# A graph convolution on one core: two chunks fetch their rows before the branch

## The chip, the cores and the metric

The kernel runs on one core of a Trainium2 chip. The metric is the device time in microseconds (us) from the kernel's start to its end on that core. The engines are called PE (TensorE, matmuls), DVE (VectorE), ACT (ScalarE), POOL (GpSimd) and SP (SyncE). Each has its own queue of instructions and works through it in order; they wait for each other by semaphores. SP, ACT and POOL also issue DMA transfers.

## The reference

Two graph convolutions with attention over 6250 nodes of 128 features and 106250 edges sorted by destination, a batch normalisation with ReLU between them, and a layer norm of the sum with x at the end. Each edge has 64 attributes, a weight that serves as a time, and a source whose node has a time of its own:

```python
def _transformer_conv(h, edge_attr, src, dst, ...):
    q, k, v = (h @ Wq + bq), (h @ Wk + bk), (h @ Wv + bv)      # each (n, H=2, C=64)
    e = (edge_attr @ We).reshape(-1, H, C)
    kj = k[src] + e
    alpha = einsum('ehc,ehc->eh', q[dst], kj) / sqrt(C)
    ex = exp(alpha - segment_max(alpha, dst)[dst])
    a = ex / segment_sum(ex, dst)[dst]
    out = segment_sum((v[src] + e) * a[:, :, None], dst)
    return out.reshape(n, H * C) + h @ Ws + bs

rel_t = last_update[src] - t                                    # node_vec[src] - edge_weight
edge_attr = concatenate([cos(rel_t[:, None] * time_w + time_b), msg], axis=-1)
h = relu(batch_norm(_transformer_conv(x, edge_attr, ..conv 1..)))
return layernorm(x + _transformer_conv(h, edge_attr, ..conv 2..))
```

## The kernel before, in words

The edges are cut into 104 chunks of 1024 (`NC`, `CE`), each of 8 tiles of 128 edges (`T`). Since the edges are sorted, a chunk's destinations lie in a window of 64 nodes (`NN`), in four groups. A tile `ff` of a chunk holds, for each edge, the source's time (column 0), the source's 128 features, 32 encoded times, 64 attributes and 16 bits that mark the destination.

The program has a plan and a branch. The plan (`tile_gnn_resnorm`, L1355 to L1521) loads source and destination indices as rows, checks that the edges are sorted and narrow enough (the result is `oki`, L1505), loads all features into SBUF (`load_features`), writes them back to DRAM with the node's time in front as `xv_d` (`pass_features`, L530 to L533), turns index rows into columns (`columns`, L1428 to L1434: `srcs`, `dsts`, `ew`), multiplies weights (`matrices`, L583 to L604), and makes the first block of the table of queries and skips (`tables`, L630 to L642, from `x0`). DVE works in this order: source columns, plan check, destination columns, matrices, table, edge weight columns. Then every engine reads `oki` and branches: `ordered` if the plan holds, `general` otherwise, which doesn't run here.

`ordered` first turns all features (`turn_features`, L656 to L662: 13 groups of transposes by PE, evacuated alternately by DVE and ACT), then runs `conv(0)` and `conv(1)`. In `conv` the order of all instructions is written out by hand, round by round; round k works on several chunks at once:

- `fetch` (L777 to L807) issues on SP the loads of a chunk ahead: attributes, tables, skips; DVE writes the bits.
- `gather` (L815) issues on POOL, per tile of the chunk, one indirect DMA of 128 rows: of `xv_d` in the first convolution, of the first one's output in the second. `bring` calls it; from round -1 on most of the eight gathers have `behind`, an extra wait for a step of PE in the same round. In the first convolution chunk k + 4 (`AHEAD`) is fetched and gathered in round k, so rounds -4 to -2 gather chunks 0 to 2 without such a wait.
- `encode` and `sine` (L853 to L867) make the encoded times of chunk k + 2 from column 0 of `ff` and the edge weights.
- `turn_in` (L885 to L897) transposes chunk k + 1; `score` (L916) makes the scores of chunk k; `lowest` (L924) takes their minimum, one instruction a round; `weigh`, `turn_weights`, `gather_sums` (L956) and `divide` to `complete` finish the chunks before.
- `pull(extra, n)` takes n steps of side work from a generator (`rest`): further blocks of the table, the second convolution's matrices, storing of outputs.

The chunk tiles `ff` come from a pool of 7 in the first convolution and of 6 in the second.

Of the kernel before, what the change touches and what calls it, by code (L numbers as in the profile page):

```python
# [15 lines left out]
H = 2  # L16
# [48 lines left out]
SWITCH = NC - 3  # L65
STARTS = (*range(0, NC - 2, LG), NC - 2, NC - 1)
# [3 lines left out]
def general(ctx: ExitStack, tc: tile.TileContext, x, src, dst, edge_attr_64, edge_weight, node_vec,  # L70
# [95 lines left out]
    step = RW * GT * (-(-64 // GT))  # L166
# [147 lines left out]
    def conv(c, kv_d, qt_d, agg_d):  # L314
        we = wt[c][4]
        w = 2 * D + (c == 1)
        with ExitStack() as cs:
            load = cs.enter_context(tc.tile_pool(name=f"load{c}", bufs=3))
# [327 lines left out]
def turn_features(nc, pl, mp, N):  # L646

    xT = pl.xT
    NF = pl.rows.shape[1]
    nc.vector.memset(xT[:, N:], 0.0)  # L650
    lanes = xT[:, :NF * P].rearrange("d (p b) -> d b p", b=NF)
    for b0 in range(0, NF, 4):
        n = min(4, NF - b0)
        px = mp.tile([P, 4, P], F32, name="fpx")
        for i in range(n):
            nc.tensor.transpose(px[:, i], pl.rows[:, b0 + i, 1:], pl.ident)  # L656
        eng = nc.scalar.copy if b0 // 4 % 2 else nc.vector.tensor_copy
        eng(lanes[:, b0:b0 + n], px[:, :n])
    if N > NF * P:
        px = mp.tile([P, 4, P], F32, name="fpx")  # L660
        nc.tensor.transpose(px[:, 0], pl.rest[:, 1:], pl.ident)
        nc.vector.tensor_copy(xT[:, NF * P:N], px[:, 0, :N - NF * P])  # L662
# [3 lines left out]
def ordered(ctx: ExitStack, tc: tile.TileContext, pl, x, dst, edge_attr_64, conv2, bn_g, bn_b, out):  # L666
# [9 lines left out]
    const = ctx.enter_context(tc.tile_pool(name="fconst", bufs=1))  # L676
    dram = ctx.enter_context(tc.tile_pool(name="fdram", bufs=1, space=bass.MemoryType.DRAM))
# [51 lines left out]
    AHEAD = 4  # L729

# [9 lines left out]
    def conv(c, extra, first_blocks=None):  # L740
# [27 lines left out]
        def fetch(k):  # L768
# [9 lines left out]
            s.f = f = load.tile([P, T, FW], F32, name="ff")  # L778
# [31 lines left out]
        def gather(k, rows, behind=None):  # L810
            f = ch[k].f
            for t in rows:
                if k == NC - 1 and t > whole:
                    continue
                row = nc.gpsimd.indirect_dma_start(  # L815
                    out=f[:, t, (1 if c else 0):1 + D], out_offset=None, in_=(h_d[:N, :] if k < RAW else hn_d) if c else pl.xv_d,
                    in_offset=bass.IndirectOffsetOnAxis(ap=pl.srcs[:, t, k:k + 1], axis=0))
# [26 lines left out]
        def encode(k):  # L844
# [8 lines left out]
            nc.vector.tensor_sub(rel, s.f[:, :, 0], pl.ew[:, :, k])  # L853
# [205 lines left out]
        with cs, tc.manual_schedule():  # L1059
            ended = None  # L1060
            for k in range(-lead(-NC), NC - 2 if c else NC + 3):
# [138 lines left out]
    with tc.tile_pool(name="fpw", bufs=2) as pw:  # L1200
        with tc.tile_pool(name="ftp", bufs=3, space=bass.MemoryType.PSUM) as mp, tc.manual_schedule():
            turn_features(nc, pl, mp, N)

# [34 lines left out]
        def rest():  # L1238
# [4 lines left out]
            others = second()  # L1243
            targets()
# [99 lines left out]
def tile_gnn_resnorm(ctx: ExitStack, tc: tile.TileContext, x, src, dst, edge_attr_64, edge_weight, node_vec,  # L1344
# [11 lines left out]
    with tc.tile_pool(name="plan", bufs=1) as pl, tc.tile_pool(name="planw", bufs=2) as mw, \  # L1356
# [4 lines left out]
        nc.gpsimd.memset(got.hT[:, N // P * (1 + D):], 0.0)  # L1361
        got.rest = keep.tile([P, 1 + D], F32, name="fxrest")
# [30 lines left out]
        got.bs1 = load_column(nc.scalar, keep, "fbs1", conv1["bs"])  # L1393
        got.wv = [keep.tile([P, D], F32, name=f"fwv{c}") for c in (0, 1)]
# [30 lines left out]
        def columns(t, to):  # L1425
# [4 lines left out]
            for t0 in range(0, T, 4):  # L1430
# [3 lines left out]
                nc.vector.tensor_copy(to[:, t0:t0 + 4], pt)  # L1434

        columns(srows, srcs)
        passed = pass_features(nc, got, made, N)

# [60 lines left out]
        x0 = pl.tile([P, GE // P, D], F32, name="fx0")  # L1499
        nc.scalar.dma_start(x0, x[:GE, :].rearrange("(b p) d -> p b d", p=P))  # L1500
        rows(nc.scalar, erows, edge_weight, CE)
# [58 lines left out]
```

## Time and profile before

| | us |
|---|---|
| median of 3 runs | 2671.73 (2668.62 to 2673.74) |
| profiled execution | 2670.95 |
| its span, first to last instruction | 2669.1 |
| PE busy | 1851.4 |
| POOL busy | 1588.3 |
| DVE busy | 1148.0 |
| ACT busy | 1082.5 |

A row of the profile's timeline gives start and duration in us from the span's start, the engine (PEld is PE's weight load; SPq and ACTq are DMA issues of these queues), the line, the operation, the tile written and the tiles read, the shape and how often; the brackets hold the idle time of the engine before it and what ended it. "issue" means that the profile shows nothing that it waited for, "remote" a releaser that the profile doesn't know. A group's row gives busy time and the mean in ns of one.

### The profile page before, as it was taken

The numbers are of one execution on the slowest core, as the hardware profiler recorded it, in microseconds if no ns is written. First come the engines' busy times: TensorE is split into PE (matmuls) and PEld (weight loads), VectorE is DVE, ScalarE is ACT, GpSimd is POOL, SyncE is SP. The second block draws the span as 40 slices with busy tenths as digits, with TensorE's granted clock in tenths as the row PEclk, the third lists the DMA queues.
The fourth block names the chain that finished last, engine by engine and source line by source line (L and its number), as shares of the span: only waits on it lengthen the run. The fifth ranks groups of instructions, "written<-read, shape, count | busy, mean of one in ns | idle before, by whom it ended". The sixth has DMA issues, their size and how long they took to land. (4 is left out here: it accounts for less than half of the span.)

```text
span 2669.1 us, 50291 instructions
## 1 busy us (share of the span) xinstructions
PE 1851.4 (69%) x14961; PEld 1107.9 (42%) x14961; DVE 1148.0 (43%) x3998; ACT 1082.5 (41%) x1906; POOL 1588.3 (60%) x1684
## 2 busy tenths in 40 slices
PE   3677767777777677677746667676767767676666
PEld 2444444444444444444424334444444434443443
DVE  3555555555555555565625222333232322232223
ACT  1455545553434444454532333333333333333333
POOL 4466666666666666666345666666666666666662
PEclk8799889988989989889977888888888898888888
DMA  6455555555555555555447555555555555555542
GB/s 177 128 148 146 146 153 145 144 143 151 146 147 138 152 148 145 144 144 138 126 118 194 148 140 148 152 153 147 143 150 148 157 147 142 154 143 140 128 134 52
DMA packets 535244, 383.29 MB, mean 144 GB/s; under 512 B 405638, under 2 KB 479258, under 8 KB 531634
## 3 DMA queue, kind: packets, MB, share of 16 engines
q1 hardware_dynamic: 460998, 231.66, 33.4%
q0 software_dynamic: 53184, 109.45, 17.1%
q10 hardware_dynamic: 20780, 38.87, 3.9%
q8 instruction: 122, 2.00, 0.3%
q14 instruction: 160, 1.31, 0.2%
HBM read 267.85 MB, written 108.49 MB: 141 GB/s over the span
## 5 line engine op out<-in xcount | busy, mean ns | idle before, releaser
L815 POOL DMA_INDIRECT ff<-xv_d,fsrcs x831 | 795.1, 957 | 511.2 <-issue 166.2
L815 POOL DMA_INDIRECT ff<-hn_d,fsrcs x783 | 743.6, 950 | 453.3 <-issue 172.3
L941 ACT COPY fpt<-fppt 128x384 f32<-128x384 f32 x208 | 99.6, 479 | 1261.9 <-PE fpx L885 705.6
L916 PE MATMUL fps<-fft,ftab 128*32 128x384 f32 (+2 forms) x2080 | 406.2, 498 | 146.5 <-issue 64.5
L956 PE MATMUL fpa<-ff,fpt 128*32 128x225 f32 x5008 | 350.6, 419 | 120.0 <-DVE fres L1032 102.2
L924 DVE TENSOR_REDUCE flow<-fps 128x1 f32<-128x384 f32 x208 | 116.1, 558 | 587.6 <-PE fpx L885 352.7
L885 PE MATMUL fpx<-fident,ff 128*128 128x128 f32 x1664 | 276.9, 299 | 38.5 <-issue 25.8
L956 PEld LDWEIGHTS fpa<-ff,fpt 128*32 128x32 f32 x5008 | 167.6, 125 | 321.0 <-issue 233.7
L916 PEld LDWEIGHTS fps<-fft,ftab 128*32 128x32 f32 x2080 | 142.7, 124 | 323.6 <-issue 161.8
L894 PE MATMUL fpe<-fident,ff 128*112 128x128 f32 x832 | 142.4, 295 | 189.0 <-issue 184.3
L889 ACT COPY fft<-fpx 128x512 f32<-128x512 f32 x404 | 232.2, 575 | 45.7 <-remote 20.1
L885 PEld LDWEIGHTS fpx<-fident,ff 128*128 128x128 f32 x1664 | 221.0, 156 | 54.5 <-issue 36.1
L916 PE MATMUL fps<-fxT,ftab 112*32 112x384 f32 (+2 forms) x1040 | 218.4, 509 | 17.2 <-issue 16.8
L963 DVE TENSOR_SCALAR finv<-fpa 128x1 f32<-128x1 f32 x208 | 32.0, 154 | 446.8 <-PE fps L916 237.6
L916 PE MATMUL fps<-fet,ftab 112*32 112x384 f32 (+2 forms) x1040 | 167.4, 448 | 33.0 <-issue 32.7
L894 PEld LDWEIGHTS fpe<-fident,ff 128*112 128x112 f32 x832 | 97.1, 141 | 218.6 <-issue 213.1
L978 PE MATMUL fpa<-fsel,fa 128*128 128x128 f32 x416 | 103.3, 332 | 81.5 <-DVE fsel L968 46.5
L860 DVE SCALAR_TENSOR_TENSOR farg<-fturns,farg 128x256 f32<-128x256 f32 x312 | 132.9, 426 | 10.7
L895 ACT COPY fet<-fpe 112x512 f32<-112x512 f32 x208 | 124.6, 599 | 9.9 <-PE fps L916 2.8
L940 PE MATMUL fppt<-fident,fs 128*128 128x128 f32 x626 | 117.1, 296 | 13.4 <-issue 5.8
L931 ACT ACTIVATE fs<-fps,fm 128x384 f32<-128x384 f32 x208 | 120.5, 579 | 9.7 <-DVE fm L926 6.1
L867 ACT ACT_TABLE_LOAD x82 | 105.2, 1283 | 42.2 <-issue 34.7
(224 smaller groups left out, 2654.4 us busy)
## 6 DMA issues: line engine op xcount, KB each, us to landing
ff<-in_edge_attr SPq DMA_DIRECT2D x206, 256.0 KB
et_d<-fet SPq DMA_DIRECT2D x104, 448.0 KB
fxT<-et_d SPq DMA_DIRECT2D x104, 448.0 KB
tab_d<-fo ACTq DMA_DIRECT2D x26, 1024.0 KB
ftab<-tab_d SPq DMA_DIRECT2D x832, 32.0 KB
enc_d<-fzs SPq DMA_DIRECT2D x104, 128.0 KB
fz<-enc_d SPq DMA_DIRECT2D x104, 128.0 KB
ff<-xv_d,fsrcs POOLq DMA_INDIRECT x831
```

Source lines behind the costliest of these rows:

```text
L815: row = nc.gpsimd.indirect_dma_start(out=f[:, t, (1 if c else 0):1 + D], out_offset=None, in_=(h_d[:N, :] if k < RAW else hn_d) if c else ...
L860: nc.vector.scalar_tensor_tensor(arg, turn, -part, arg, op0=OP.mult, op1=OP.add)
L867: nc.scalar.activation(z[:, :len(of)], arg[:, :len(of)], AF.Sin, bias=qpi)
L885: last = nc.tensor.transpose(px[:, t * P:(t + 1) * P], s.f[:, u * 4 + t, 1:1 + D], ident)
L889: nc.scalar.copy(s.ft[:, u * GE:(u + 1) * GE], px)
L894: last = nc.tensor.transpose(pe[:EC, t * P:(t + 1) * P], s.f[:, u * 4 + t, 1 + D:], ident)
L895: nc.scalar.copy(s.et[:, u * GE:(u + 1) * GE], pe[:EC])
L916: steps.append(nc.tensor.matmul(s.ps[r, to:to + n], s.tab[:kd, r, i], (of.et if i else of.ft)[:kd, at:at + n], start=i == 0, stop=i == 1))
L924: nc.vector.tensor_reduce(low, s.ps, AX.X, OP.min)
L931: nc.scalar.activation(s.s[:, :s.ps.shape[1]], s.ps, AF.Exp, bias=s.bias, scale=-1.0)
L940: last = nc.tensor.transpose(pp[:, t * P:(t + 1) * P], s.s[:, t * P:(t + 1) * P], ident)
L956: steps.append(nc.tensor.matmul(s.pa[r], s.pt[:, t * P + g * GH:t * P + (g + 1) * GH], f[:, i % T, 1:1 + D + EW], start=t == 0, stop=t == ...
```

## The change

Chunks 0 and 1 (`EARLY`) get tiles of their own, allocated for the whole program. As soon as the source columns stand, POOL gathers their 16 tiles of rows from x itself, so without the node's time, ahead of the branch and of `xv_d`. `gather` then leaves these two out.

The times that are missing are picked in the plan by `early_times`. node_vec lies in 98 rows of 64 (`SLOT`). For each of the 2 x 1024 edges PE spreads the source index over 98 lanes, ACT squares its distance from each lane's centre, DVE compares, which gives a one-hot column; PE multiplies it with node_vec's rows, and DVE multiplies with a one-hot of the low six bits and sums. This goes in 4 units (2 chunks x 2 halves of 512 edges), one after each of the first four steps of `tables`. `encode` reads the result for these chunks.

In the plan DVE now does the check, then the matrices, the preparation of the picked times, the code, the table with the units between its steps, the edge weight columns and the destination columns last. The load of `x0` on ACT's queue moves up, ahead of the loads of edge weights.

`turn_features` no longer stands ahead of the first round: it is a generator at the head of the side work, of which 3 steps are taken in rounds -2 and -1 and 7 more in round 0. In the first convolution gathers have no `behind` up to round 2, so chunks 3 to 6 are gathered without PE's pace as well. The other five chunk tiles are allocated once, in two pools (`upper` for chunks 2 and 3, `lower` for 4 to 6), and both convolutions use the ring of 7. Two buffer sizes in `general` shrink.

```diff
+AHEAD = 4
+EARLY = 2
+SLOT = 64
...
+def early_times(nc, pl, keep, plan, mw, rowf, node_vec, wide):
+
+    N = node_vec.shape[0]
+    n = -(-N // SLOT)
+    of = plan.tile([P, SLOT], F32, name="fslots")
+    nc.vector.memset(of[n // 32 * 32:], 0.0)
+    nc.scalar.dma_start(of[:N // SLOT], node_vec[:N // SLOT * SLOT].rearrange("(p b) -> p b", b=SLOT))
+    if N % SLOT:
+        nc.scalar.dma_start(of[n - 1:n, :N % SLOT], node_vec[N // SLOT * SLOT:].rearrange("(a b) -> a b", a=1))
+    centre = plan.tile([P, 2], F32, name="fcentre")
+    nc.vector.tensor_copy(centre[:, 0:1], pl.lanes)
+    nc.vector.tensor_scalar(centre[:, 1:2], centre[:, 0:1], -float(SLOT), 0.5 - SLOT / 2, op0=OP.mult, op1=OP.add)
+    row = plan.tile([EARLY, P], F32, name="frow")
+    nc.vector.tensor_copy(row, pl.ident[:EARLY, 1:2].to_broadcast([EARLY, P]))
+    low = plan.tile([P, T, EARLY], I32, name="flowi")
+    nc.vector.tensor_scalar(low, pl.srcs[:, :, :EARLY], SLOT - 1, None, op0=OP.bitwise_and)
+    lowf = plan.tile([P, T, EARLY], F32, name="flowf")
+    nc.vector.tensor_copy(lowf, low)
+    times = pl.early_times = keep.tile([P, EARLY, T], F32, name="fearly")
+    yield
+    for k in range(EARLY):
+        at = plan.tile([P, T, SLOT], F32, name=f"fat{k}")
+        nc.vector.tensor_tensor(at, lowf[:, :, k:k + 1].to_broadcast([P, T, SLOT]),
+                                pl.place_of[:, None, :SLOT].to_broadcast([P, T, SLOT]), OP.is_equal)
+        for u in range(CE // GE):
+            ps = wide()
+            nc.tensor.matmul(ps[:n], (row if k else pl.ones)[:k + 1, :n], rowf[:k + 1, u * GE:(u + 1) * GE], start=True, stop=True)
+            near = mw.tile([P, GE], F32, name="fnear")
+            nc.scalar.activation(near[:n], ps[:n], AF.Square, bias=centre[:n, 1:2])
+            nc.vector.tensor_scalar(near[:n], near[:n], SLOT * SLOT / 4.0, None, op0=OP.is_lt)
+            pv = wide().rearrange("p (t b) -> p t b", b=P)
+            for i in range(GT):
+                nc.tensor.matmul(pv[:, i, :SLOT], near[:n, i * P:(i + 1) * P], of[:n], start=True, stop=True)
+            t = slice(u * GT, (u + 1) * GT)
+            nc.vector.tensor_mul(at[:, t], at[:, t], pv[:, :, :SLOT])
+            nc.vector.tensor_reduce(times[:, k, t], at[:, t], AX.X, OP.add)
+            yield
...
-def turn_features(nc, pl, mp, N):
+def turn_features(nc, pl, N):
...
-        px = mp.tile([P, 4, P], F32, name="fpx")
+        px = pl.bank().rearrange("p (b d) -> p b d", d=P)
...
+        yield
...
+    lower, upper = (ctx.enter_context(tc.tile_pool(name=f"fring{i}", bufs=1)) for i in (0, 1))
+    more = [(upper if i < 2 else lower).tile([P, T, FW], F32, name=f"ff{i}") for i in range(AHEAD + 3 - EARLY)]
+    pl.ffs = pl.early + more
...
-            s.f = f = load.tile([P, T, FW], F32, name="ff")
+            s.f = f = pl.ffs[k % len(pl.ffs)]
...
             f = ch[k].f
+            if not c and k < EARLY:
+                return
...
-            nc.vector.tensor_sub(rel, s.f[:, :, 0], pl.ew[:, :, k])
+            nc.vector.tensor_sub(rel, pl.early_times[:, k] if k < EARLY else s.f[:, :, 0], pl.ew[:, :, k])
...
-                        gather(j, rows, behind)
+                        gather(j, rows, behind if c or k > 2 else None)
...
+                if not c and k in (-2, -1):
+                    pull(extra, 3)
                 if k >= 0:
                     at_round[0] = k
+                    if k == c == 0:
+                        pull(extra, 7)
...
-        with tc.tile_pool(name="ftp", bufs=3, space=bass.MemoryType.PSUM) as mp, tc.manual_schedule():
-            turn_features(nc, pl, mp, N)
...
             others = second()
+            yield from turn_features(nc, pl, N)
             targets()
...
+        got.early = [keep.tile([P, T, FW], F32, name=f"ffe{k}") for k in range(EARLY)]
...
-        columns(srows, srcs)
+        srowf = columns(srows, srcs)
+        for k in range(EARLY):
+            for t in range(T):
+                nc.gpsimd.indirect_dma_start(out=got.early[k][:, t, 1:1 + D], out_offset=None, in_=x,
+                                             in_offset=bass.IndirectOffsetOnAxis(ap=srcs[:, t, k:k + 1], axis=0))
         passed = pass_features(nc, got, made, N)
-
+        timed = early_times(nc, got, keep, pl, mw, srowf, node_vec, wide)
+        made_ready = matrices(nc, got, 0, keep, bank, pl)
...
-        columns(drows, dsts)
-
-        for _ in matrices(nc, got, 0, keep, bank, pl):
+        rows(nc.scalar, erows, edge_weight, CE)
+        for _ in made_ready:
             pass
+        next(timed)
         codes(nc, got, keep, mw, bank)
...
-        for _ in tables(nc, got, 0, xT0, 0, mw, wide):
+        made_table = tables(nc, got, 0, xT0, 0, mw, wide)
+        for _ in range(2 * H):
+            next(made_table)
+            next(timed, None)
+        for _ in made_table:
+            pass
+        for _ in timed:
             pass
         columns(erows, ew)
+        columns(drows, dsts)
```

More of the change, by code (lines that the diff above doesn't have):

```diff
@@ L165, in general @@
     span = G * GE // P * RW
-    step = RW * GT * (-(-64 // GT))
+    step = RW * GT * (-(-48 // GT))
     zeros = op.tile([P, step], F32, name="zeros")
@@ L317, in conv @@
         with ExitStack() as cs:
-            load = cs.enter_context(tc.tile_pool(name=f"load{c}", bufs=3))
+            load = cs.enter_context(tc.tile_pool(name=f"load{c}", bufs=2))
             work = cs.enter_context(tc.tile_pool(name=f"work{c}", bufs=3))
@@ L658, in turn_features @@
         eng(lanes[:, b0:b0 + n], px[:, :n])
+        yield
     if N > NF * P:
-        px = mp.tile([P, 4, P], F32, name="fpx")
-        nc.tensor.transpose(px[:, 0], pl.rest[:, 1:], pl.ident)
-        nc.vector.tensor_copy(xT[:, NF * P:N], px[:, 0, :N - NF * P])
+        px = pl.bank()[:, :P]
+        nc.tensor.transpose(px, pl.rest[:, 1:], pl.ident)
+        nc.vector.tensor_copy(xT[:, NF * P:N], px[:, :N - NF * P])
+        yield
 @with_exitstack
@@ L727, in targets @@
         nc.vector.scalar_tensor_tensor(target, none, float(P), target, op0=OP.mult, op1=OP.add)
-    AHEAD = 4
     SINGLE, LATE = 43, 85
@@ L1393, in tile_gnn_resnorm @@
         got.bs1 = load_column(nc.scalar, keep, "fbs1", conv1["bs"])
+        x0 = pl.tile([P, GE // P, D], F32, name="fx0")
+        nc.scalar.dma_start(x0, x[:GE, :].rearrange("(b p) d -> p b d", p=P))
         got.wv = [keep.tile([P, D], F32, name=f"fwv{c}") for c in (0, 1)]
@@ L1498, in tile_gnn_resnorm @@
         nc.vector.tensor_copy(wrong, pb)
-        x0 = pl.tile([P, GE // P, D], F32, name="fx0")
-        nc.scalar.dma_start(x0, x[:GE, :].rearrange("(b p) d -> p b d", p=P))
-        rows(nc.scalar, erows, edge_weight, CE)
         tot = pl.tile([1, 1], F32, name="tot")
```

1 line of the change is left out of this document (added).

## The prediction

> **What bounds the kernel now.** I read the page's first part, then its groups, then the start in order of time, because the change touches only the start and the row gathers.
>
> ```profile
> span 2669.1 us, 50291 instructions
> PE 1851.4 (69%) x14961; PEld 1107.9 (42%) x14961; DVE 1148.0 (43%) x3998; ACT 1082.5 (41%) x1906; POOL 1588.3 (60%) x1684
> L815 POOL DMA_INDIRECT ff<-xv_d,fsrcs x831 | 795.1, 957 | 511.2 <-issue 166.2
> ```
>
> Over the whole span PE leads, and POOL's gathers come next. What the change can win lies in the first 90 us. From the timeline (start, duration, engine, line, operation; in brackets the idle time before it and what ended it):
>
> ```profile
> 11.23 1.28 DVE L1434 CAST fsrcs<-fpx 128x416 int32<-128x416 f32 x2 [1.05 <-PE fpx L1433]
> 24.59 0.14 DVE L1505 TENSOR_SCALAR oki<-tot 1x1 int32<-1x1 f32 x1
> 33.61 1.11 POOL L815 DMA_INDIRECT ff<-xv_d,fsrcs  x1 [30.16 <-DMA fwv<-in_L_gnn_Wv]
> 35.02 0.94 POOL L815 DMA_INDIRECT ff<-xv_d,fsrcs  x1 [0.31 <-issue]
> 36.27 0.94 POOL L815 DMA_INDIRECT ff<-xv_d,fsrcs  x1 [0.30 <-issue]
> 35.59 4.51 PE L630 MATMUL fpx<-fxT,fm 128*128 128x512 f32 x6 [0.78 <-DVE fxT L1515]
> 41.66 1.13 DVE L638 SCALAR_TENSOR_TENSOR fo<-fpx,fb,fcode 128x512 f32<-128x512 f32 x1 [0.40 <-PE fpx L630]
> 44.73 0.59 DVE L1434 COPY few<-fpx 128x416 f32<-128x416 f32 x1 [0.67 <-PE fpx L1433]
> 50.25 0.21 DVE L791 TENSOR_TENSOR fbits<-fdsts,fbitm 128x64 int32<-128x64 int32 x1
> 67.31 1.01 DVE L658 COPY fxT<-fpx 128x512 f32<-128x512 f32 x1 [16.86 <-issue]
> 67.47 0.94 POOL L815 DMA_INDIRECT ff<-xv_d,fsrcs  x1 [0.30 <-issue]
> 68.38 1.57 PEld L656 LDWEIGHTS fpx<-fident,fhT 128*128 128x128 f32 x8 [17.44 <-issue]
> 72.93 1.88 ACT L658 COPY fxT<-fpx 128x512 f32<-128x512 f32 x2 [14.36 <-remote]
> 79.41 1.02 ACT L658 COPY fxT<-fpx 128x512 f32<-128x512 f32 x1 [0.68 <-PE fpx L656]
> 80.22 0.43 DVE L854 TENSOR_TENSOR farg<-frel,ftw 128x256 f32<-128x256 f32 x1
> 90.24 0.56 DVE L924 TENSOR_REDUCE flow<-fps 128x1 f32<-128x384 f32 x1 [1.50 <-PE fps L916]
> ```
>
> The source indices stand in columns at 12.5 us, but POOL's first gather begins at 33.6. From there gathers come every 1.25 us without a pause until 68.4. The plan ends on DVE at 45.3 (44.73 + 0.59). From about 50.4 to 72.9 DVE, PE and ACT then stand almost still, though little stands in their way: I call this the freeze. Chunk 0 gets its first row minimum at 90.2. Is the freeze bound to the gathers? Busy time by stretches (first the plan under gathers, then the freeze, then the same at the start of the second convolution) and the rows around the end of that one:
>
> ```profile
> 33.60:48.00 14.40, 11.31 (x35) 5.90 (x35) 4.42 (x6) 3.02 (x3) 11.04 (x12) 0.92 0.50 155
> 50.00:67.00 17.00, 1.11 (x4) 0.71 (x4) 0.46 (x4) 1.01 (x1) 13.04 (x14) 0.50 0.28 60
> 1351.00:1363.00 12.00, 9.69 (x36) 5.65 (x36) 4.20 (x7) 10.12 (x14) 8.88 (x10) 0.77 0.48 163
> 1376.00:1394.00 18.00, 4.71 (x31) 2.44 (x28) 0.69 (x1) 3.42 (x4) 13.73 (x15) 0.62 0.49 134
> 1368.50 0.94 POOL L815 DMA_INDIRECT ff<-h_d,fsrcs  x1 [1.38 <-remote]
> 1393.46 0.94 POOL L815 DMA_INDIRECT ff<-h_d,fsrcs  x1 [0.30 <-issue]
> 1398.12 1.29 DVE L1222 COPY fhn<-fpg 128x512 f32<-128x512 f32 x2 [8.40 <-remote]
> ```
>
> The columns are PE, PE loads, DVE, ACT and POOL busy, the granted clock, the DMA share, GB/s. Both times an unbroken run of gathers first does no harm (11.31 us of PE in 14.4, 9.69 in 12), then the other engines hardly issue (1.11 in 17, 4.71 in 18), and they come back some 4 us after the run's last gather (68.4 to 72.9; 1394.4 to 1398.1). I take from this: grace of 14.8 us from the run's start (33.6 to 48.4, a little after the undisturbed window), then a freeze until 4 us after its end, in which a quarter of the work gets through (4.71/18; in the first one less).
>
> **The change part by part.**
>
> *Early gathers.* The 16 gathers of chunks 0 and 1 need only the source columns. They start at 12.6 instead of 33.6 and last 16 x 1.25 = 20 us, to 32.6, beside the plan check. Their 1 MB comes on top of the plan's loads; I cost that at nothing, since oki at 24.6 is wanted by POOL only at 32.6 (if that cover is gone, POOL merely pauses). By grace and tail this run freezes 12.6 + 14.8 = 27.4 to 36.6: 9.2 us, of which three quarters are lost: +7. Ends: 0, and 9.2.
>
> *ACT's queue.* x0's load moves ahead of the edge weights there, and two loads of node_vec (25 KB) come behind the copies of the weights, ahead of the first picked time. Nothing on ACT waits for them before the tables; a load of this size that came 3 us late would add those 3 us to the picked times, inside the ends given below.
>
> *Next run.* POOL then passes the branch and gathers chunks 2 and 3, which need all of xv_d. That was complete when the gather began at 33.6 and may come some 3 us later now, so I start it at 37: 16 gathers to 57, freeze 51.8 to 61: +7. Chunks 4 to 6 go to buffers of the lower ring; I assume that these lie where plan tiles lay, and that POOL waits there for the plan's end.
>
> *Picked times.* Four units are added on the chain PE, ACT, DVE, PE, DVE, with the nearest rows:
>
> ```profile
> L630 PE MATMUL fpx<-fxT,fm 128*128 128x512 f32 x8 | 5.6, 844 | 1.2 <-DVE fxT L1515 0.8 <-issue 0.4
> L633 ACT ACTIVATE fskip<-fpx,fbs 128x512 f32<-128x512 f32 x1 | 0.7, 687 | 2.9 <-DVE fo L638 2.9
> L1434 DVE COPY few<-fpx 128x416 f32<-128x416 f32 x2 | 1.2, 592 | 1.3 <-PE fpx L1433 1.3
> L1433 PE MATMUL fpx<-fident,erows 104*128 104x104 f32 x8 | 1.2, 267 | 1.1 <-issue 0.7 <-DVE fo L638 0.4
> L658 DVE COPY fxT<-fpx 128x512 f32<-128x512 f32 x4 | 4.1, 1023 | 7.2 <-remote 4.7 <-PE fpx L656 2.5
> ```
>
> One unit: the row spread by PE, 2 x 0.84 = 1.7; Square 0.7; the compare up to 0.6; eight small matmuls, 8 x 0.2 = 1.6 (under the 0.267 of the wider row); product and sum 2 x 0.4. That is 5.4 with nothing overlapped. The table step that alternates with it took 1.8 ((42.8 - 35.6)/4), and some 1.4 of it can lie under the unit, so 4 a unit, 16 in all, and 1 for the preparation: +17. Ends: 7 (DVE's part alone is on the path) and 24 (nothing overlaps, clock as low as in the freeze, and the two PSUM buffers make every step wait). Sent ahead of them, the weights gain what the destination columns lose; that move is worth nothing, because both end before DVE reaches the branch.
>
> *Turned features.* Between 72.9 and 80.4 the kernel only turned the remaining features. These 13 groups now come out of the side work, 3, 3 and 9 steps in rounds -2 to 0. -6.5 in front; DVE keeps 7 copies of 1.02 in its queue ahead of chunk 0 and 1, of which I charge +5 (0 if all lie under encoding on ACT and PE; 7 if none).
>
> *The old freeze* goes: -22.
>
> *Last run.* When the plan lets go of its tiles, POOL sends 24 gathers (chunks 4 to 6) in 30 us without TensorE's pace, where they were paced before. Freeze 30 - 14.8 + 4 = 19 us in round 0, three quarters lost: +14. Ends: 0, and 19.
>
> *Rounds 0 to 2* then hold no gathers. Rows of the minimum, first with gathers at the start, then over 1000 us, then at the end of the first convolution, without gathers:
>
> ```profile
> L924 DVE TENSOR_REDUCE flow<-fps x3: 557/557/558, 106.3 to 128.8; 128x1 f32<-128x384 f32 x3
> 200.00:1200.00 1000.00, 45.70 (x82) 0.91 0.56 146
> L924 DVE TENSOR_REDUCE flow<-fps x3: 547/547/550, 1310.8 to 1327.5; 128x1 f32<-128x384 f32 x3
> ```
>
> 11.25 us a round at the start, 12.2 later, 8.35 without gathers. Two steps of side work remain in these rounds, so I take 2.3 of the 2.9 for three rounds: -7 (0 to -9). From round 3 on the old pace holds, and the rest of the kernel is as before. The second convolution gets 7 chunk buffers for 6; its first gather of a round waits for the last sum of the round before anyway, so 0 (ends -3 and +3, a quarter of a microsecond on a dozen rounds).
>
> Sum: 7 + 7 + 17 - 6.5 + 5 - 22 + 14 - 7 = +14.5. The profiled execution took 2670.95, 0.8 below the median of 2671.73; 2671 + 14 = **2685**.
>
> [...] The instruction queues show nothing in the freeze (these are all queues that moved anything from 50 to 70):
>
> ```profile
> q0 software_dynamic: 513, 1.06, 24.8%
> q1 hardware_dynamic: 432, 0.10, 2.2%
> ```
>
> [...]
>
> **The rivals.**
> 1. *No new freeze* (faster). If the freeze needs something that only the old order brings, such as SP's table loads meeting the gathers, then 7, 7 and 14 fall away: -14, 2657. For it: the first 14 us of each run did no harm. Against it: two freezes with the same tail.
> 2. *Freeze only behind the branch*: 7 + 7 fall away, 14 stays: 0, 2671. For it: the plan ran undisturbed under 12 gathers.
> 3. *POOL does not pause after chunk 3* because the lower ring does not touch late plan tiles: one run of 40, 37 to 87, frozen 51.8 to 91, 39 x 0.75 = 29 in place of 7 + 14: +22, 2693. It decides when chunk 4's gather starts before the picked times end.
> 4. *The freeze belongs to the branch*: it stays, no other comes: -6.5 + 5 + 17 - 7 = +8.5, 2679.
>
> **How the numbers follow.** Forecast 0.40, rivals 0.24, 0.16, 0.12 and 0.08. A measurement of this kernel cannot tell less than about 0.2%, 5 us, from no change. Faster: rival 1 and a quarter of rival 2, 0.28. Same: half of rival 2 and a little of the forecast and of rival 4, 0.13. Slower: the rest, 0.59. The range takes in rivals 1 and 3 for the most part, 2655 to 2698; the forecast's own, by the ends of the picked times and the runs, is 2674 to 2697.
>
> **What would show it.** In the changed profile: the first gather near 12.6; stretches after some 27 in which DVE, PE and ACT hardly issue; the plan's end on DVE near 76 (45.3 + 17 + 7 + 7) where it was 45.3; the gathers of chunks 4 to 6 unbroken, with a freeze behind them in round 0; rounds 1 and 2 under 10 us; rounds of 12.2 afterwards. I am wrong if the minimum of chunk 0 stands before 80, if the picked times take under 8 us, or if the second convolution's rounds move.

## The result

The changed kernel takes 2679.21 us (median of 19 runs), the kernel before, run beside it on the same chip, 2670.41 (19 runs): a ratio of 1.0029, 95% interval 1.0019 to 1.0038. The change costs some 8 us.

The head of the page of the changed kernel, and its costliest group of gathers (591 of them write the ring's tiles, the rest the two early tiles):

```profile
span 2678.7 us, 48976 instructions
PE 1875.1 (70%) x15001; PEld 1132.7 (42%) x15001; DVE 1157.5 (43%) x4018; ACT 1084.6 (40%) x1910; POOL 1587.0 (59%) x1684
L862 POOL DMA_INDIRECT ff<-xv_d,fsrcs x591 | 564.0, 954 | 348.7 <-issue 126.4
```

PE's busy time rose by 24 us, DVE's by 10, the others' by 2 or less; most of the difference lies in when things happen. The timeline of the changed kernel's start, DVE and POOL with one row of PE, with the steps the prediction named:

```profile
11.76 1.11 POOL L1492 DMA_INDIRECT ffe<-in_x,fsrcs  x1 [8.31 <-DVE fsrcs L1486]
27.36 0.14 DVE L1560 TENSOR_SCALAR oki<-tot 1x1 int32<-1x1 f32 x1
35.37 0.94 POOL L862 DMA_INDIRECT ff<-xv_d,fsrcs  x1 [3.06 <-DMA xv_d<-fhT]
40.98 2.08 PE L672 MATMUL fpx<-fxT,fm 128*128 128x512 f32 x2 [0.78 <-DVE fxT L1570]
48.70 0.42 DVE L575 TENSOR_REDUCE fearly<-fat 128x4 f32<-128x256 f32 x1
58.32 0.42 DVE L575 TENSOR_REDUCE fearly<-fat 128x4 f32<-128x256 f32 x1
71.16 0.42 DVE L575 TENSOR_REDUCE fearly<-fat 128x4 f32<-128x256 f32 x1
75.93 1.09 DVE L1486 CAST fdsts<-fpx 128x416 int32<-128x416 f32 x2 [0.73 <-PE fpx L1485]
76.99 0.94 POOL L862 DMA_INDIRECT ff<-xv_d,fsrcs  x1 [21.77 <-DVE fdsts L1486]
105.94 0.94 POOL L862 DMA_INDIRECT ff<-xv_d,fsrcs  x1 [0.30 <-issue]
110.84 1.01 DVE L700 COPY fxT<-fpg 128x512 f32<-128x512 f32 x1 [22.38 <-remote]
112.35 0.55 DVE L971 TENSOR_REDUCE flow<-fps 128x1 f32<-128x384 f32 x1
129.12 0.56 DVE L971 TENSOR_REDUCE flow<-fps 128x1 f32<-128x384 f32 x1 [3.31 <-PE fps L963]
136.99 0.55 DVE L971 TENSOR_REDUCE flow<-fps 128x1 f32<-128x384 f32 x1
145.66 0.56 DVE L971 TENSOR_REDUCE flow<-fps 128x1 f32<-128x384 f32 x1 [0.26 <-PE fppt L987]
157.79 0.56 DVE L971 TENSOR_REDUCE flow<-fps 128x1 f32<-128x384 f32 x1 [4.14 <-remote]
2660.63 0.68 DVE L971 TENSOR_REDUCE flow<-fps 128x1 f32<-128x512 f32 x1
```

The gathers begin 21.8 us earlier than before. POOL has finished four chunks by about 55, then stands 21.8 us and waits for the plan's last instruction on DVE, as it must if the next chunk's tile lies where plan tiles lay. The plan ends at 77.0, before it was 45.3. Then 24 gathers run without a pause to 106.9, DVE does nothing for 22.4 us, and chunk 0's row minimum stands at 112.4 instead of 90.2. The two rounds from 129.1 to 145.7 take 7.9 and 8.7 us.

The same in stretches (the columns are PE, PE loads, DVE, ACT and POOL busy, the granted clock, the DMA share, GB/s), the start of the run of 24 gathers and what followed:

```profile
77.00:88.50 11.50, 6.81 (x32) 6.60 (x33) 10.35 (x36) 3.71 (x5) 8.76 (x10) 0.65 0.40 87
88.50:110.80 22.30, 7.19 (x30) 2.98 (x28) 0.00 (x0) 2.59 (x4) 14.12 (x15) 0.58 0.30 67
```

First DVE is busy 10.4 of 11.5 us beside the gathers, then 0 of 22.3. This is the freeze, in a place where the kernel before had none.

The distance to the kernel before is +22.1 us at chunk 0 (112.35 - 90.24), +15.5 at chunk 4 (157.79 against 142.30), +16.0 at the last minimum of the first convolution, and +9.9 at the last minimum (2660.63 against 2650.74).

### The profile page after: what moved, and what is told of

Read it like the earlier page. It is cut to its first block, busy times and chain, and to the rows that moved or that the text cites. A ratio compares the mean times of both kernels' runs of the same rounds, so it can differ in the third digit from the quotient of the medians.

```text
span 2678.7 us, 48976 instructions
## 1 busy us (share of the span) xinstructions
PE 1875.1 (70%) x15001; PEld 1132.7 (42%) x15001; DVE 1157.5 (43%) x4018; ACT 1084.6 (40%) x1910; POOL 1587.0 (59%) x1684
## 4 chain that ended last, share of the span: by engine, by line
PE 48%; issue 19%; DVE 11%; ACT 10%; another core or an unknown queue 7%; DMA 2%; SPq 2%; POOL 0%; ACTq 0%; DVEq 0%; POOLq 0%
PE fps L963 15%; PE fpx L932 7%; PE fpa L1003 6%; PE fpg L672 4%; PE fpe L941 3%; PE fpa L1025 3%; PE fppt L987 2%; PE fpa L1026 2%; ACT fft L936 2%; ACT L1086 2%; ACT L1089 2%; PE fpa L1040 1%; PE fpa L1041 1%; DVE fa L1013 1%
## 5 line engine op out<-in xcount | busy, mean ns | idle before, releaser
L862 POOL DMA_INDIRECT ff<-xv_d,fsrcs x591 | 564.0, 954 | 348.7 <-issue 126.4
L862 POOL DMA_INDIRECT ff<-hn_d,fsrcs x559 | 530.0, 948 | 324.4 <-issue 125.7
L1003 PE MATMUL fpa<-ff,fpt 128*32 128x225 f32 x3564 | 271.7, 417 | 78.9 <-DVE fres L1079 45.8
L862 POOL DMA_INDIRECT ffe<-xv_d,fsrcs x224 | 213.9, 955 | 165.0 <-PE fps L963 66.2
L862 POOL DMA_INDIRECT ffe<-hn_d,fsrcs x224 | 213.6, 953 | 126.4 <-issue 51.6
L1010 DVE TENSOR_SCALAR finv<-fpa 128x1 f32<-128x1 f32 x208 | 32.3, 155 | 456.8 <-PE fps L963 205.8
L1003 PEld LDWEIGHTS fpa<-ff,fpt 128*32 128x32 f32 x3564 | 122.4, 125 | 243.3 <-issue 170.3
L932 PE MATMUL fpx<-fident,ff 128*128 128x128 f32 x1184 | 199.8, 303 | 34.3 <-issue 26.5
L941 PE MATMUL fpe<-fident,ff 128*112 128x128 f32 x592 | 101.7, 298 | 120.6 <-issue 119.7
L932 PEld LDWEIGHTS fpx<-fident,ff 128*128 128x128 f32 x1184 | 161.5, 159 | 44.2 <-issue 35.1
L1003 PE MATMUL fpa<-ffe,fpt 128*32 128x225 f32 x1444 | 118.8, 406 | 16.5 <-DVE fres L1079 12.5
```

The costliest lines, as they stand in the source:

```text
L862: row = nc.gpsimd.indirect_dma_start(out=f[:, t, (1 if c else 0):1 + D], out_offset=None, in_=(h_d[:N, :] if k < RAW else hn_d) if c else ...
L932: last = nc.tensor.transpose(px[:, t * P:(t + 1) * P], s.f[:, u * 4 + t, 1:1 + D], ident)
L941: last = nc.tensor.transpose(pe[:EC, t * P:(t + 1) * P], s.f[:, u * 4 + t, 1 + D:], ident)
L1003: steps.append(nc.tensor.matmul(s.pa[r], s.pt[:, t * P + g * GH:t * P + (g + 1) * GH], f[:, i % T, 1:1 + D + EW], start=t == 0, stop=t == ...
```

## The experiments

One thing has to be known first: the runs fell on several chips. Experiments 1 to 4 ran on chip 0, where the kernel before takes 2671.7 us. Experiments 5 to 8 ran on chip 4, 9 and 10 on chip 5, 11 and 12 on chip 14; there the kernel before takes 2204.7, 2206.3 and 2204.8 us. For the result above no chip is on record; the kernel before took 2670.4 us beside it, so I count it with chip 0. Each ratio is to the kernel before on the same chip.

**1. TensorE's pace back** (chip 0).

```diff
-                        gather(j, rows, behind if c or k > 2 else None)
+                        gather(j, rows, behind)
```

> The changed kernel, with the row gathers of chunks 3 to 6 in the first convolution waiting for steps of TensorE again, as before the change; everything else stays. My theory (a run of gathers without a pause stops the other engines, here from 88.5 to 110.8 us) expects no freeze behind the plan: chunk 0's row minimum comes some 15 us earlier, near 97, rounds 1 and 2 go back to about 11 us because the gathers lie in them again, so the kernel is 7 to 12 us faster than the changed one (2667 to 2672). Rival: the stop belongs to something else at the plan's end (the branch, the start of the table's loads); then chunk 0's minimum stays near 112 and the time is 2679 or, with rounds of 11 us, up to 2686.

2672.98 us, ratio 0.9999 (0.9988 to 1.0010): faster than the changed kernel by 8 us going by the two ratios, by 6 going by the medians. From its timeline, the plan's end, a gather of round -1, and the minima of chunks 0 and 4:

```profile
76.45 1.28 DVE L1486 CAST fdsts<-fpx 128x416 int32<-128x416 f32 x2 [1.11 <-PE fpx L1485]
89.02 1.02 POOL L862 DMA_INDIRECT ff<-xv_d,fsrcs  x1 [0.69 <-DVE farg L907]
94.70 0.56 DVE L971 TENSOR_REDUCE flow<-fps 128x1 f32<-128x384 f32 x1 [3.07 <-PE fpe L941]
153.03 0.56 DVE L971 TENSOR_REDUCE flow<-fps 128x1 f32<-128x384 f32 x1 [3.28 <-PE fpx L932]
```

The plan ends where it did, yet chunk 0's minimum comes 17.7 us earlier: the stop behind the plan hangs on the unbroken gathers and not on the branch or the plan's end. The rounds carry gathers again and take back most of it, so chunk 4 gains only 4.8. My theory expected some 97 and 2667 to 2672; it came out 2 us earlier at the minimum and 1 us beyond the slow end of the time.

**2. Six chunk tiles in the second convolution** (chip 0).

```diff
-            s.f = f = pl.ffs[k % len(pl.ffs)]
+            s.f = f = pl.ffs[k % (6 if c else len(pl.ffs))]
```

> The changed kernel with the second convolution using 6 of the 7 chunk tiles, as before the change. The changed kernel was 15 us behind at the end of the first rounds but only some 10 behind at the end. If the seventh tile brought those 5 us, this one takes 2684 and its loss against the kernel before stays at 14 to 15 through the second convolution. If the 5 us are only scatter between executions, it takes 2679.

2675.48 us, ratio 1.0018 (1.0006 to 1.0031). It is not slower than with seven tiles, so the seventh brought nothing that shows. The distance to the profile of before falls here too, from 10.2 us at the end of the first convolution to 4.6 at the last minimum. Up to there its program is that of the changed kernel, so it also shows the scatter between two executions: the plan ends at 74.7 instead of 77.0, and chunks 0 and 4 are 18.6 and 12.6 us behind the kernel before where the changed kernel was 22.1 and 15.5 behind.

**3. No picked times** (chip 0). The times of the sources of chunks 0 and 1 stay zero, so this kernel leaves out a part of the work.

```diff
-    for k in range(EARLY):
-        at = plan.tile([P, T, SLOT], F32, name=f"fat{k}")
-...
-            nc.vector.tensor_reduce(times[:, k, t], at[:, t], AX.X, OP.add)
-            yield
+    nc.vector.memset(times, 0.0)
+    yield
```

> The changed kernel without the four units of picked times: the times of the sources of chunks 0 and 1 are left at zero, so their encodings are not the reference's, and nothing else is left out. My sum put 17 us on the units, the trace of the changed kernel shows about 7 us for each of the four steps, of which 1.8 are the table's own. If they are on the path whole, the plan ends 20 to 23 us earlier, at 54 to 57, and the kernel takes 2656 to 2659. Rival: POOL's gathers of chunks 2 and 3 end at 55 anyway and run then without a pause into those of chunks 4 to 6, one run of 40 gathers with a longer freeze, so that half of it or more is lost again: 2665 to 2672.

2664.95 us, ratio 0.9980 (0.9969 to 0.9991): 13 us below the changed kernel by the ratios, at the edge of what the rival gave and 6 us above what I expected. Its timeline around the plan's end and the freeze:

```profile
59.45 0.59 DVE L1471 CAST fdsts<-fpx 128x416 int32<-128x416 f32 x1 [5.71 <-remote]
60.16 0.94 POOL L847 DMA_INDIRECT ff<-xv_d,fsrcs  x1 [3.48 <-issue]
90.47 1.01 DVE L685 COPY fxT<-fpg 128x512 f32<-128x512 f32 x1 [18.83 <-issue]
94.19 0.56 DVE L956 TENSOR_REDUCE flow<-fps 128x1 f32<-128x384 f32 x1 [2.12 <-PE fpx L917]
```

The plan ends 17.0 us earlier (60.04 against 77.02). It would be more, but the other engines now stop behind the gathers of chunks 2 and 3: DVE stands 4.1 us before the first half of the destination columns and 5.7 before the second. The freeze of the 24 gathers moves along with the plan's end and is only a little shorter, 18.8 us. So the time falls by most of the 17 us. What the rival had right is the loss in the plan; one run of 40 gathers did not form.

This run also shows a condition that my theory lacks. The changed kernel sends the same 16 gathers at the same time (35.4 to 55.2, here 37.0 to 56.7), but there nothing stops. The same stretch, first in the changed kernel, then without picked times, and then SP's two neighbouring issues in the changed kernel and the one in this run:

```profile
50.00:59.00 9.00, 6.41 (x14) 2.96 (x14) 1.53 (x4) 1.85 (x2) 4.00 (x5) 1.00 0.16 37
50.00:59.00 9.00, 0.07 (x1) 0.00 (x0) 0.59 (x1) 0.00 (x0) 5.16 (x6) 0.55 0.39 97
35.72 0.38 SPq L826 DMA_DIRECT2D ffe<-in_edge_attr  x1
70.65 1.93 SPq L842 DMA_DIRECT2D ftab<-tab_d  x4
50.20 7.10 SPq L827 DMA_DIRECT2D ftab<-tab_d  x4
```

PE works 6.41 of 9 us against 0.07. A dense run of gathers is not enough, then. In the changed kernel SP had nothing to issue from 36 to 70; here it issues table loads, and it has loads in every other stop too: from 47.0 in the kernel before, from 90.4 in the changed one (2 us after the stop began), and in the second convolution of before four from 1362.7 that take 4.1 us, while PE works 0.87 us between 1363 and 1368. Loads early in a run did no harm (78.2 to 82.6 in the changed kernel, where DVE is busy 10.4 of the 11.5 us around them). That is the condition of rival 1, SP's loads meeting the gathers. It is not shown to be the cause: SP's issue is itself slowed in each stop (four table loads take 9.0, 9.8, 7.1 and 4.1 us there, and 1.98 right behind the stop of the changed kernel), and no run moves these loads alone.

**4. Gathers spaced in the kernel before** (chip 0). A clearing of a spare tile on POOL follows every gather of chunks 0 to 3.

```diff
+    pl.idle = const.tile([P, 464], F32, name="fidle")
 ...
+                if not c and k < 4:
+                    nc.gpsimd.memset(pl.idle, 0.0)
```

> The kernel before the change, with one clearing of a spare tile on POOL (some 0.48 us) behind every gather of chunks 0 to 3 in the first convolution, so that gathers come every 1.7 us and not every 1.25 us. If the freeze from 50 to 72 us hangs on gathers without a pause, it goes or shrinks, chunk 0's row minimum comes 10 to 18 us earlier than at 90.2, and the kernel takes 2653 to 2661. If the freeze belongs to the branch, it stays: 2670, or some us more because the gathers of chunk 3 end later. If only the number of gathers in a run counts and not their spacing, the run is longer (28 times 1.7 = 48 us, to 81) and the freeze lasts to 85: 2680 or more.

2675.93 us, ratio 1.0020 (1.0011 to 1.0030): slower, by a fault of mine. From its timeline, POOL first, then SP's and DVE's part of the time in which the kernel before was frozen:

```profile
47.60 0.48 POOL L823 MEMSET fidle<- 128x464 f32 x1 [13.57 <-DMA skip_d<-fskip]
48.28 0.95 POOL L816 DMA_INDIRECT ff<-xv_d,fsrcs  x1 [0.20 <-issue]
49.89 0.95 POOL L816 DMA_INDIRECT ff<-xv_d,fsrcs  x1 [0.16 <-issue]
58.89 1.97 SPq L798 DMA_DIRECT2D ftab<-tab_d  x4
78.77 0.54 DVE L927 TENSOR_REDUCE flow<-fps 128x1 f32<-128x384 f32 x1
87.37 0.17 DVE L856 TENSOR_TENSOR frel<-ff,few 128x8 f32<-128x8 f32 x1 [7.87 <-DMA ff<-xv_d,fsrcs]
```

The spare tile lay over a tile that the plan still sent out, so POOL stood 13.6 us behind the first gather and the others came 13 us late. All the same chunk 0's minimum stands at 78.8, 11.5 us earlier than in the kernel before. From 48.3 on the gathers run without any pause, one every 1.61 us, to beyond 99, and no freeze comes. The clearest stretch is late in the run, 39 us after its start:

```profile
48.30:63.00 14.70, 8.41 (x41) 7.20 (x41) 8.41 (x20) 6.80 (x7) 13.24 (x19) 0.73 0.50 107
87.30:97.00 9.70, 3.71 (x22) 1.41 (x26) 8.27 (x30) 1.79 (x2) 8.73 (x13) 0.50 0.44 98
```

DVE is busy 8.3 of 9.7 us as soon as its rows have landed (the wait of 7.87 ends with a gather). So on this chip the harm came with dense gathers: at 1.25 us apart they stopped the others, at 1.61 they didn't, although SP issued its table loads all the while (some 2.0 us for four). The branch, which is unchanged here, is not enough. The run also starts later than in the kernel before, behind the branch; but so does the last run of the changed kernel, which freezes. The time was lost because the first rounds now waited for late and slow gathers.

**5 to 7. Spacing without that fault** (chip 4). The spare tile lies among the long-lived ones; 5 is the kernel before with 384 columns, 6 has 256 and the turned features as side work besides, 7 is the changed kernel with experiment 1's edit and 256 columns, behind the early gathers too.

```diff
+    got.idle = keep.tile([P, 384], F32, name="fidle")
 ...
+                if not c and k < 4:
+                    nc.gpsimd.memset(pl.idle, 0.0)
```

> The kernel before the change with spaced gathers again (a clearing of a spare tile on POOL behind every gather of chunks 0 to 3), but the spare tile now lies where it overlaps nothing, so that POOL doesn't wait for the plan's last transfer (47.6 us in the run with spaced gathers before this one), and it is smaller: 384 columns, some 0.4 us. By my theory the freeze stays away and the gathers start at 33 us again: chunk 0's row minimum at 72 to 80 where it was 90.2, chunk 4's at 133 to 137 where it was 142.3, 2656 to 2664. If the freeze stays away but the gathers, now slower, become what the first rounds wait for, chunk 4's minimum stays near 142 and the time near 2671. If the freeze comes back with the earlier start, its cause is not the spacing: 2671 or more.

> The kernel before the change, with two edits: the features are turned as side work in rounds -2 to 0, as the change has it, and the gathers of chunks 0 to 3 are spaced by a smaller clearing (256 columns, some 0.3 us, a gather every 1.4 us). No early gathers and no picked times. By my theory no freeze comes, the first chunk doesn't wait for the turned features, and the kernel is 3 to 7 us faster than with the spacing alone: 2650 to 2660. Rival: a gather every 1.4 us is still too dense, a freeze stands behind the run, and the time is 2665 to 2672.

> The changed kernel with TensorE's pace for chunks 3 to 6 again (as in the run with the pace alone) and, besides, a clearing of 256 columns behind every gather of chunks 0 to 3, the early ones too. The run with the pace alone was level with the kernel before and its plan's check ended at 31.3 us. By my theory the early runs cost 7 and 7 us there, so this one is 5 to 12 us faster than it, 2660 to 2667, and the check ends near 25. If only the freeze behind the branch is real, it stays at 2671 to 2674.

2215.73 us (1.0047, 1.0034 to 1.0061), 2213.97 (1.0039, 1.0025 to 1.0053) and 2219.74 (1.0065, 1.0051 to 1.0079), beside 2204.74 for the kernel before. All three are slower, by 0.4 to 0.7%, and all my expectations missed. (In 7 most of it is the change's own loss, see 11.) The next run tells why.

**8. The kernel before, unchanged** (chip 4).

> The kernel before the change, unchanged, profiled a second time. All five kernels so far seem to regain 4 to 6 us on the profile of before in the second convolution, also the one whose second convolution is that of before. If that lies in the one profiled execution of before, this profile shows the same regain of some 4 us against it; if it lies in the kernels, this profile follows the first one within a us or two.

2203.85 us. Windows of this execution, the same as in the prediction's table of before:

```profile
33.60:48.00 14.40, 11.31 (x34) 6.03 (x35) 4.61 (x8) 3.03 (x3) 11.05 (x12) 0.92 0.48 147
50.00:67.00 17.00, 10.35 (x57) 8.67 (x61) 13.93 (x36) 8.98 (x12) 13.04 (x14) 0.78 0.57 127
```

POOL sends the same run of gathers (13.04 us and 14 of them in the second window, on chips 0 and 4), yet DVE works 13.93 us there, where it was 0.46 on chip 0. There is no freeze. Rows of its timeline:

```profile
47.45 2.48 SPq L797 DMA_DIRECT2D ftab<-tab_d  x4
69.48 0.56 DVE L924 TENSOR_REDUCE flow<-fps 128x1 f32<-128x384 f32 x1 [1.09 <-PE fps L916]
107.80 0.55 DVE L924 TENSOR_REDUCE flow<-fps 128x1 f32<-128x384 f32 x1
```

And its rounds later in the first convolution (one minimum a round):

```profile
200.00:1000.00 800.00, 43.49 (x79) 0.87 0.68 176
```

79 rounds in 800 us are 10.1 us a round, and eight gathers at 1.25 us are 10.0; DVE waits 188.5 us in 78 waits for gathered rows to land, on chip 0 0.4 us in 2. So here the rounds follow POOL's gathers, and spacing them costs time, as 5 and 6 show. What I wanted of this run, the scatter between two profiles of before on chip 0, it can't give.

**9. The turned features alone** (chip 5). The kernel before with `turn_features` as side work, as the change has it.

```diff
-        with tc.tile_pool(name="ftp", bufs=3, space=bass.MemoryType.PSUM) as mp, tc.manual_schedule():
-            turn_features(nc, pl, mp, N)
 ...
             others = second()
+            yield from turn_features(nc, pl, N)
 ...
+                if not c and k in (-2, -1):
+                    pull(extra, 3)
```

> The kernel before the change with one part of the change alone: the features are turned as side work, 3, 3 and 9 steps in rounds -2 to 0; gathers, plan and everything else as before. My sum gave this part -6.5 in front and +5 in the queues of chunks 0 and 1. Where the kernel before takes 2671 us, the run of 28 gathers and its freeze stay, so 2666 to 2672. Where the kernel before takes 2205 us (no freeze there, the gathers at 1.25 us are the bound from the start), the first round can't start earlier than its gathers allow and the time stays within 3 us of 2205.

2206.41 us, ratio 1.0002 (0.9993 to 1.0011). Against the profile of experiment 8, which is of another chip with the same time, chunk 0's minimum comes 6.0 us earlier (63.45), those of chunks 1 to 5 some 2.5 to 3.4 us, and at chunk 6 0.9 are left, since the gathers bound the rounds. As expected.

**10. and 12. The same with spaced gathers** (chips 5 and 14, 256 columns). It is the kernel of experiment 6 again, meant for chip 0, where it was never run.

```diff
+    got.idle = keep.tile([P, 256], F32, name="fidle")
 ...
+                if not c and k < 4:
+                    nc.gpsimd.memset(pl.idle, 0.0)
```

> The same with the gathers of chunks 0 to 3 spaced by a clearing of 256 columns on POOL (one every 1.4 us), which the earlier call could only try on a chip without the freeze. Where the kernel before takes 2671 us: if the freeze hangs on gathers at their densest, it goes, chunk 0's row minimum comes at 60 to 70 and chunk 4's at 115 to 130, and the kernel takes 2650 to 2661; if 1.4 us is still too dense, a freeze stands between 50 and 80 and the time is 2664 to 2672. Where the kernel before takes 2205 us: 2213 to 2215 again, since every spaced gather only delays the bound.

> Turned features as side work and gathers of chunks 0 to 3 at 1.4 us, a third time, in case this call comes to a chip with the freeze. Where the kernel before takes 2671 us: no freeze if it hangs on gathers at their densest, chunk 0's row minimum at 60 to 70, chunk 4's at 115 to 130, 2650 to 2661; with a freeze left 2664 to 2672. Where it takes 2205 us: 2211 to 2215.

2212.39 us (1.0025, 1.0014 to 1.0036) and 2212.75 (1.0035, 1.0022 to 1.0049), as expected for a chip without the freeze, the first by 0.6 us below its range. Whether spacing from 33 us on beats both kernels on chip 0 was not tried.

**11. The changed kernel, unchanged** (chip 14).

> The changed kernel, unchanged, beside the kernel before on one chip once more. Where the kernel before takes 2205 us there is no freeze and the gathers at 1.25 us are the bound: the plan still ends some 32 us later than before (near 77) and chunk 0's row minimum comes 15 to 20 us later than at 69.5; the 24 gathers of chunks 4 to 6 then run without harm to the others and rounds 1 and 2 are short, so that I expect +4 (POOL starts chunk 4 at 77, where the kernel before starts it at 73.4) to +16 (as with the pace and the spacing), 2209 to 2221. Where the kernel before takes 2671 us: 2677 to 2681, with the freeze behind the run of 24 gathers as in the first profile.

2215.41 us, ratio 1.0046 (1.0030 to 1.0061): slower by 10 us here too, without any freeze. The time and chunk 0's minimum are as expected; the plan's end came at 70.3, not near 77. Its timeline, then the 22.3 us that answer to the frozen ones above, again from 11.5 us after the start of the run of 24 gathers (70.3 to 100.4):

```profile
24.23 0.14 DVE L1560 TENSOR_SCALAR oki<-tot 1x1 int32<-1x1 f32 x1
35.26 2.08 PE L672 MATMUL fpx<-fxT,fm 128*128 128x512 f32 x2 [0.78 <-DVE fxT L1570]
69.24 1.09 DVE L1486 CAST fdsts<-fpx 128x416 int32<-128x416 f32 x2 [0.73 <-PE fpx L1485]
70.30 0.95 POOL L862 DMA_INDIRECT ff<-xv_d,fsrcs  x1 [14.89 <-DVE fdsts L1486]
85.68 0.56 DVE L971 TENSOR_REDUCE flow<-fps 128x1 f32<-128x384 f32 x1 [1.02 <-PE fps L963]
```

```profile
81.80:104.10 22.30, 17.03 (x122) 10.99 (x121) 14.32 (x46) 13.31 (x19) 14.28 (x15) 0.79 0.71 165
```

With it the change can be taken apart, since chips 4 and 14 show the same steps undisturbed:

| us | before, chip 0 | changed, chip 0 | before, chip 4 | changed, chip 14 |
|---|---|---|---|---|
| oki | 24.6 | 27.4 | 25.0 | 24.2 |
| table's first matmul | 35.6 | 41.0 | 36.0 | 35.3 |
| plan's end on DVE | 45.3 | 77.0 | 45.5 | 70.3 |
| minimum of chunk 0 | 90.2 | 112.4 | 69.5 | 85.7 |
| minimum of chunk 4 | 142.3 | 157.8 | 107.8 | 126.8 |

## Why the prediction was right

The forecast was 2685, +14 us; the measurement is 2679, +8. Sign and place came out, and most of the mechanism: the old freeze goes, a new one comes behind the last run, and the picked times hold up the plan. Several terms were off, in opposite directions, and the end of the kernel gave back more than I allowed. That the sum still lies near is partly luck.

*Early gathers, +7.* The table's first matmul stands at 41.0, against 35.3 undisturbed: 5.7 us, of which 3.1 were lost before oki. In experiments 1 and 2, with the same plan, it stands at 42.2 and 39.0, so the term is 4 to 7. The first gather at 11.8 and the end of the run at 32.3 are as worked out.

*Next run, +7.* This step failed. From the table's start to the plan's end the changed kernel takes 36.0 us on chip 0 and 35.1 on chip 14: the 16 gathers of chunks 2 and 3 cost 1 us, not 7. One picked unit is stretched, 9.6 us from 48.7 to 58.3 where its fellows on chip 14 take 7.0, and the next makes up 1.2 of it (5.8). No freeze came: between 50 and 59 PE works 6.41 us, against 7.67 undisturbed. I had charged the freeze to any long run of gathers. Without the units (experiment 3) it came at the place that I gave, and cost the columns 4.1 and 5.7 us; what differs in the rows is that SP then issues its table loads in it. Which condition the freeze needs beside dense gathers stays open.

*Picked times, +17.* Too small. Undisturbed, table, units and columns take 35.1 us against 9.5, and 2.4 of that are the destination columns: some 23 us for four units, near my upper end of 24. The mis-sized part is the overlap with the table: a unit with its table step takes 7.0 us (the last units on chip 0, from 64.12 to 71.16), where I had 5.8. My unit of 5.4 and the table step of 1.8 make 7.2, so the two overlap hardly at all.

*Destination columns moved, 0.* Too small as well: oki to the table still took 11.0 us without them on chip 14, as with them on chip 4, since DVE waited longer for PE's products of the weights (6.0 us against 4.2) and prepared the picked times, and at the end the columns cost their own 2.4 us. Together the plan's end moved by 24.9 us undisturbed and by 31.7 on chip 0; I said 31, from wrong parts.

*Turned features, -6.5 and +5.* Experiment 9 shows -6.0 at chunk 0 and -2.5 at chunk 1, -2.9 at chunk 4: right, the +5 a little high. Undisturbed, chunk 0's minimum follows the plan's end 8.7 us sooner than before (24.0 to 15.4); what of that is more than these 6.0 my sum lacks.

*The old freeze, -22.* Chunk 0's minimum came 44.9 us after the plan's end on chip 0 and 24.0 on chip 4: 20.9. The tail of 4 us was read off ACT alone: in the kernel before DVE resumed at 67.3 and PE at 68.4, with the run's last gather.

*Last run, +14, and rounds without gathers, -7.* From the plan's end to chunk 0's minimum the change takes 35.3 us with the freeze and 15.4 without: 20, where I had 14 for 19 us at three quarters; here nothing of DVE's work came through. From chunk 0's minimum to chunk 4's the change then wins back 6.6 (+22.1 to +15.5). Net of both, experiment 1 measures 6 to 8 us, I had 7.

So the loss at the start was +15.5 against a predicted +14.5, and +12.6 in the second execution of the same plan (experiment 2). The last step, that the rest of the kernel stays as before, failed by some 6 us: the changed kernel's profile regains that much from the end of the first convolution on (+16.0 to +9.9). The ring is not the reason (experiment 2). The four other kernels on chip 0 regain 4 to 10 us on this profile of before, also experiment 4, whose second convolution is the old one. It may lie in that one execution of the kernel before. It stays open.

The rivals: 1 (no new freeze) is false on chip 0; on chip 14 no freeze comes, but on chip 4 the old one is missing too, and the change still loses. The condition that it names, SP's loads meeting the gathers, fits every stop and was not tested. 2 (only behind the branch) is half true: the runs inside the plan cost 6.7 us of 14. 3 is false, POOL waited 21.8 us. 4 (the freeze belongs to the branch) gave 2679, the very time that was measured, yet it falls with experiments 1 and 4, which have the same branch and no freeze behind it, and with experiment 8: a time alone doesn't tell the mechanisms apart. No run shows a freeze that the branch alone brings.

What was missing from all of them: that the freeze is not a property of the program. I had derived a law from two stops in one execution. It held for some dense runs of gathers on chip 0, not for the second run of the changed kernel, and for none on chips 4 and 14.

## What to carry to other kernels

Before work is moved to an idle engine, price what the move puts on the chain that others wait for: here two chunks fetched 22 us earlier cost some 23 us of small dependent steps, and the engine that had been helped stood 21.8 us waiting for those steps. A stall in which nothing is waited for may belong to the chip and not to the program (here 22.3 us in the changed kernel on chip 0, none on chip 14); profile the same program on another chip before building on it or against it. Where a run of indirect DMAs does disturb the others, a pace (a wait for a step of the engine that consumes the rows) removed the disturbance here (chunk 0's minimum came 17.7 us earlier). Spacing the gathers cost 0.25 to 0.5% on the chips where they are the bound; what the pace alone costs there was not run.

## What the runs showed of the hardware

One program took 2671 us on chip 0 and 2205 on chips 4, 5 and 14. Instructions of POOL and ACT take the same time on chip 0 and chip 4: a gather 957 and 961 ns, the feature copy of ACT 575 and 579. PE, whose ends are modelled, shows 1851 and 1653 us busy. The granted clock was 0.879 and 0.860, so the faster chip has not the higher one. The rest of the difference is idle time, much of it such that an engine waits for nothing that the profile shows. The same group of PE on chip 0 (kernel before):

```profile
L894 PE MATMUL fpe<-fident,ff 128*112 128x128 f32 x832 | 142.4, 295 | 189.0 <-issue 184.3
```

and on chip 4:

```profile
L894 PE MATMUL fpe<-fident,ff 128*112 128x128 f32 x832 | 159.6, 326 | 3.8 <-DVE ff L872 3.8
```

184 us against next to nothing, and rounds of 12.2 against 10.1 us. Rounds without gathers are alike: the changed kernel's two take 7.9 and 8.7 us on chip 0, 7.9 and 8.3 on chip 14. So chip 0 loses its time beside the gathers. That its bound there is not PE, as the busy share suggests, but how the engines get to issue, is my reading and not shown.

In a freeze SP is slow too: four table loads whose issue takes 2.0 us took 9.0 in the freeze of the kernel before and 9.8 in that of the changed one:

```profile
93.24 9.83 SPq L842 DMA_DIRECT2D ftab<-tab_d  x4
112.54 1.98 SPq L842 DMA_DIRECT2D ftab<-tab_d  x4
```

So POOL's queue goes on and the four others nearly stop together (in the changed kernel, in 22.3 us, POOL is busy 14.1 with 15 gathers, DVE not at all, PE 7.2 and ACT 2.6). On chip 0 this came with gathers 1.25 us apart and SP's loads beside them; with gathers 1.61 us apart none came in 50 us, and none came in the second run of the changed kernel, beside which SP loaded nothing. Why chip 0 does this and the others not, and whether it is the chip or something else that differed between the runs, no run here shows.
